# Four channel chunks in two visits: regrouping the half-height products of layer 0 inside the score loop of layer 1

## The chip, the cores and the metric

The kernel runs on one core of a Trainium2 chip, as one program that is launched once. The metric is the time of one execution on the device, in microseconds (us). The core has a matrix engine (TensorE, "PE" in the profile; its weight loads are listed apart as "PEld"), a vector engine (VectorE, "DVE"), a scalar engine (ScalarE, "ACT"), GpSimd ("POOL") and DMA queues. Each engine works through its own queue in order, and semaphores tie the queues together.

## The reference, cut to what matters

The input is x, 8 images of 512 channels and 1024 pixels. Four layers follow one another. The change touches the end of layer 0 and the start of layer 1:

```python
# layer 0, per image; f, g: 64 channels after batch norm and relu, h: 64 channels
z  = einsum('bcn,bcm->bnm', f, g)
z2 = einsum('bnm,bcm->bcn', z / largest_singular_value(z), h)
x  = conv1x1(z2, Wv, bv) + x
# layer 1: group norm over 32 groups of 16 channels, then attention over 1024 pixels
h  = group_norm(x)
q, k, v = conv1x1(h, wq), conv1x1(h, wk), conv1x1(h, wv)
x  = x + conv1x1(softmax(q^T k / sqrt(512)) v, wp)
```

Layer 2 is a second attention with 128 channels, and layer 3 is a 1x1 convolution with signs, a batch norm and a parametric relu. All sums must be those of the reference in float32.

## The kernel before

**Tiling.** Channels lie on 128 partitions in `CC` = 4 chunks, pixels in `NH` = 2 halves of 512. A product has 512 columns at most and goes to one of 8 PSUM banks (`bank()`). A float32 product shows in the trace as two passes, so two MATMUL records.

**An entry stage, then a steady part.** The entry stage (to about 192 us) reads all images for the batch norm of layer 0, prepares weights and brings the first image into layer 1. The steady part is `fast(env, n, hb, ua)`, called for n = 0 to 7, one image each in the order 6, 7, 0, 1, ... 5. In it an image runs through layers 1 to 3, and the end of layer 0 for the next image is woven in.

**The end of layer 0 for the next image is `enter` (line 399).** Layer 0 has been folded so that x becomes x + pv^T f + bias, with `pv` 64 x 512 (made by `weights0`, line 283, from the 64 x 64 matrix of the chain below) and `f` 64 x 1024. Only 64 of the 128 rows of the array are needed, so pixel half 0 uses rows 0 to 63 and pixel half 1 uses rows 64 to 127 (`side(h)`). For each of the 4 channel chunks, `enter` takes two banks and issues the two half-height products (line 408); VectorE adds them to x (line 417) and takes the statistics of the sum (line 420, gathered in line 421). Then it yields, so one chunk is one *visit*. After four visits there are two small steps with products by `gmat`, which average the statistics over the groups of 16 channels: the first is line 428 (VectorE prepares it in 427 and reads it in 429 to 432), the second is line 435, followed by the reciprocal root on GpSimd and VectorE. The results are the scale and shift of the group norm, which `normal` (line 447) applies at step 5 of `values1`, half-way through the image.

**The weights need two half-height products more, for every second image.** `entering` (line 855) loads f, makes sure that the chain of the image pair is finished, and for an even image calls `weights0` for both images of the pair (line 287, with copies to the tile `pv` by VectorE in line 290 and ScalarE in line 292). It then goes straight on to the first visit.

**The score loop is the clock.** `scores1` makes the 1024 x 1024 scores as 4 blocks of `seven` products (Strassen's scheme), so the loop in `fast` has 28 steps k = 0 to 27; at each one TensorE does 4 passes of 128 x 128 x 512 (line 385). Within a block of seven, two of the banks are accumulated over two steps with others between; at k = 6, 13, 20 and 27 a block ends. VectorE evicts four products of a block (lines 342 and 344), ScalarE the others and the exponentials, and the sums of the exponentials are two VectorE additions for each block (lines 529 to 532). `make_v` follows with 14 steps of the same length, then `values1` with 14 steps (line 552).

**Work is woven in by step.** At k = 8 `entering` starts; at k = 12, 15, 18, 21, 24 and 27 (`k >= 11 and k % 3 == 0`) one step of it is drawn: four visits, then the two group products. `chore(2)` draws, every second call, one step of the *chain*: 22 small steps for each image pair, which find the largest singular value of z by repeated squaring (two products of 128 x 128 in lines 1013 and 1014, evicted by VectorE or ScalarE, now and then a sum in line 1045). The three chains left for the steady part are used up in the first images.

**Queues.** The program order is a wish: the compiler's scheduler lays out the queue of each engine by its own estimates of when an operand is ready, and moves ready work ahead of what is not. Only the entry stage keeps TensorE in the order written (`tc.manual_schedule`).

Of the kernel before, what the change touches and what calls it, by code (L numbers as in the profile page):

```python
# [20 lines left out]
CC = C // P  # L21
NT = N // P
HF = 512
NH = N // HF
# [61 lines left out]
def kernel(  # L86
# [36 lines left out]
    def bank():  # L123
        return psum["bank"].tile([P, HF], F32, tag="bank", name="bank")
# [271 lines left out]

    weights = {}

    def enter(xt, f, pv):

        st = stat.tile([P, CC, NH, 6], F32, tag="st1", name="st1")
        mv = stat.tile([P, CC, 2], F32, tag="mv1", name="mv1")
        for oc in range(CC):
            banks = [bank() for h in range(NH)]
            for h, ps in enumerate(banks):
                mm(  # L408
                    out=ps,
                    lhsT=pv[side(h), bass.ts(oc, P)],  # L410
                    rhs=f[side(h), :],
                    start=True,
                    stop=True,
                )
            for h, ps in enumerate(banks):
                xs = xt[:, oc, half(h)]
                nc.vector.scalar_tensor_tensor(
                    xs, ps, bvo[:, oc : oc + 1], xs, ALU.add, ALU.add
                )
                nc.vector.bn_stats(st[:, oc, h, :], xs)  # L420
            nc.vector.bn_aggr(mv[:, oc, :], st[:, oc, :, :])
            yield

        ps = bank()
        mean = stat.tile([P, CC], F32, tag="mean1", name="mean1")
        dev = stat.tile([P, CC], F32, tag="dev1", name="dev1")
        nc.vector.tensor_tensor(mv[:, :, 0], mv[:, :, 0], bo, ALU.subtract)
        mm(out=ps[:, 0:CC], lhsT=gmat, rhs=mv[:, :, 0], start=True, stop=True)
        nc.vector.tensor_copy(mean, ps[:, 0:CC])
        nc.vector.tensor_tensor(dev, mv[:, :, 0], mean, ALU.subtract)  # L430
        nc.vector.tensor_tensor(dev, dev, dev, ALU.mult)
        nc.vector.tensor_tensor(dev, dev, mv[:, :, 1], ALU.add)
        yield
        ps = bank()
        mm(out=ps[:, 0:CC], lhsT=gmat, rhs=dev, start=True, stop=True)
        sc = rsqrt_eps(stat, ps[:, 0:CC], CC, "r1")
        bi = stat.tile([P, CC], F32, tag="bi1", name="bi1")
        nc.vector.tensor_tensor(sc, sc, vec("L1_conv_gamma"), ALU.mult)
        nc.vector.tensor_tensor(mean, mean, bo, ALU.add)
        nc.vector.tensor_tensor(bi, mean, sc, ALU.mult)  # L440
        nc.vector.tensor_tensor(bi, vec("L1_conv_beta"), bi, ALU.subtract)
        norm[:] = sc, bi
        yield
# [411 lines left out]
    def entering(n):  # L855

        b = order[n]
        f = load_f(b)

        def steps():  # L860
            while b // 2 not in ready:
                next(behind)
            if b % 2 == 0:
                for i in (b, b + 1):
                    pvs[i] = weights0(i)
            yield from enter(resident[b], f, pvs.pop(b))

        return steps()

# [3 lines left out]
    def fast(env, n, hb, ua):  # L873


        b = order[n]
        xt = resident.pop(b)
        more = n + 1 < B
        ahead = iter(())
        count = [0]  # L880

        def chore(every):
            count[0] += 1
            if count[0] % every == 0:
                next(behind, None)

        es = [None] * NT
        for k, _ in enumerate(scores1(env, hb, ua, es)):
            if rest3 and k % 2 == 0:
                if next(rest3[0], "end") == "end":  # L890
                    rest3.pop()
                    if more and order[n + 1] not in resident:
                        resident[order[n + 1]] = load_x(order[n + 1])
            if n == 0 and k == 2:
                weights["o"] = sums_of(quarters_of(wo, chunks, cols2), [so[:, i] for i in range(3)], True)
            if n == 0 and k == 6:
                tp = quarters_of(sbw["tpg"], chunks, [slice(0, P), slice(P, 2 * P)])
                weights["tp"] = sums_of(tp, [sp[:, i] for i in range(3)], True)
            if k == 8 and more:
                ahead = entering(n + 1)  # L900
            if k >= 11 and k % 3 == 0:
                next(ahead, None)
            if not rest3:
                chore(2)
        for _ in ahead:
            pass
        esum = es.pop()
        vt = env["big"].tile([P, NT, C], F32, tag="uv", name="vt")
        for k, _ in enumerate(make_v(hb, vt)):
            if k == 3:  # L910
                r = inverse_sums(env, esum, n)
            chore(2)
        scratch = env["big"].tile([P, 3, N], F32, tag="us", name="scratch")
        got = []
        steps = iter(())
        for k, _ in enumerate(values1(env, xt, vt, es, r, scratch)):
            chore(2)
            if k == 5 and more:
                nxt = resident[order[n + 1]]
                hb = split_h(env, normal(env, nxt))  # L920
        signs = None
        if more:
            steps = make_u(env, hb, got)
        else:
            signs = unpacked(env)

        def fill(k=1):
            for _ in range(k):
                next(steps, None)

        made = []
        for k, _ in enumerate(project2(env, xt, made)):
            fill(k > 5)
        tt, pt, gt = made
        es, esum = scores2(env, pt, tt, lambda t: fill(t % 2))
        banks, r = [None, None], None

        def values2(h, ts):
            if banks[h] is None:
                banks[h] = bank()  # L940
            for t in ts:
                mm(  # L942
                    out=banks[h],
                    lhsT=gt[:, t, :],
                    rhs=es[t][:, half(h)],
                    start=t == 0,
                    stop=t == NT - 1,
                )
            if t == NT - 1:
                att = env["small"].tile([P, HF], F32, tag="half_b", name="att")  # L950
                nc.vector.tensor_tensor(att, banks[h], r[:, h, :], ALU.mult)
                return att

        dst = channels(out[b])
        fill()
        values2(0, range(0, 2))
        if more:
            r = inverse_sums(env, esum, B + n)  # L960
            values2(0, range(2, NTH))
            att = values2(0, range(NTH, NT))
            values2(1, range(0, NTH))
            close2(xt, att, 0)
            att = values2(1, range(NTH, NT))
            fill()
            for _ in leave(env, xt, dst, [0]):
                fill()
            close2(xt, att, 1)
            rest3.append(leave(env, xt, dst, [1], stop=True))  # L970
            next(rest3[0])
            fill(2)
            for _ in steps:
                pass
        else:


            r = inverse_rows(env, esum, B + n)
            att = values2(0, range(2, NT))
            values2(1, range(0, 2))  # L980
            close2(xt, att, 0)
            values2(1, range(2, 6))
            before, after = leave(env, xt, dst, [0], signs), leave(env, xt, dst, [1], signs)
            count = count_bad(env)
            next(count)
            next(before)
            next(before)
            att = values2(1, range(6, NT))
            next(before)
            close2(xt, att, 1)  # L990
            for _ in before:
                pass
            next(after)
            next(count)
            for _ in after:
                pass

        return hb, got[0] if more else None
# [435 lines left out]
    with tc.manual_schedule(engines={mybir.EngineType.PE}):  # L1434
        steps = entering(0)
        for k, _ in enumerate(chain(jl, True)):

            for _ in range(4 if k == 3 * NSTEP + 3 else 2 if k != 1 and k % 3 < 2 else 1):
                next(todo, None)
            for args in (next(relus, None),):  # L1440
                if args:
                    relu(*args)
        for k in range(CC + 2):
            next(steps)
            for _ in range(3 if k < CC else 5):
                next(todo, None)
        for _ in todo:
            pass
# [193 lines left out]
```

## Time and profile before

| | before |
|---|---|
| time, median of three (range) | 1924.97 us (1924.53 to 1925.95) |
| span of the profiled execution | 1922.7 us |
| TensorE busy | 1897.7 us, 99% |
| VectorE busy | 1136.0 us, 59% |
| ScalarE, GpSimd busy | 509.5 us, 227.3 us |
| full-height products of 512 columns in the score loop (line 385) | 4 records of a step follow one another in 1.72 us |
| half-height products of `enter` (line 408) | 128 records in 32 visits of 4 records |
| addition of line 417, statistics of line 420 | 742 ns and 688 ns, 64 of each |

The page names the busy share of each engine over the span. A MATMUL record overlaps the next one (592 ns long, but the next starts 430 ns later), so the distance from one start to the next is what a product costs; the timeline by engine gives the starts. In the timeline, a row is a group of equal records in sequence: start, length, engine, line, tile and operands, number of records, and in brackets the idle time before it and who ended it. The list of waits gives, for each pair of waiting and releasing line, the sum, the number and the longest.

### The profile page before, as it was taken

To read this page: it belongs to the slowest core of one execution; us is meant where nothing else is said; L and a number is where in the kernel's file an instruction comes from. 1 tells how busy PE (TensorE), PEld (TensorE's weight loads), DVE (VectorE), ACT (ScalarE), POOL (GpSimd) and SP (SyncE) were. 2 spreads that over 40 slices of the span, in tenths; PEclk is the share of its full clock that TensorE was granted. 3 is DMA by queue.
4 is the path that set the end of the run, shared out by engine and by line. 5 is a ranking of instruction groups with operands and counts; after the bars stand their busy time and mean duration, and the time that the engine had idled before them with its cause. 6 is when DMAs were issued, how large, how long until landed. Compare 5 with 4: busy or idle time off the path is not lost.

```text
span 1922.7 us, 16428 instructions
## 1 busy us (share of the span) xinstructions
PE 1897.7 (99%) x6166; PEld 978.9 (51%) x6166; DVE 1136.0 (59%) x1761; ACT 509.5 (27%) x811; POOL 227.3 (12%) x175
## 2 busy tenths in 40 slices
PE   9999999999999999999999999999999999999997
PEld 3376456544655446444545446544645455544653
DVE  3246577448764677447754676447653775466547
ACT  2141222035212332024212431034202521143114
POOL 0000011200111001200121011201120011101121
PEclk9999999999999999999999999999999999999999
DMA  8420000002000120002000120002000200010001
GB/s 325 150 77 7 0 6 12 1 12 88 17 1 0 33 71 12 1 11 88 17 1 0 33 71 12 1 12 88 11 0 2 96 7 6 0 34 22 12 0 46
DMA packets 27783, 66.46 MB, mean 35 GB/s; under 512 B 4272, under 2 KB 5424, under 8 KB 27056
## 3 DMA queue, kind: packets, MB, share of 16 engines
q1 hardware_dynamic: 26768, 64.90, 10.0%
q8 instruction: 51, 0.84, 0.2%
q10 hardware_dynamic: 864, 0.43, 0.1%
q14 instruction: 36, 0.29, 0.1%
q0 software_dynamic: 64, 0.00, 0.0%
HBM read 38.51 MB, written 18.87 MB: 30 GB/s over the span
## 4 chain that ended last, share of the span: by engine, by line
PE 90%; DVE 8%; ACT 1%; issue 1%; DMA 0%; POOL 0%; DVEq 0%; ACTq 0%
PE bank L385 40%; PE bank L552 20%; PE bank L942 6%; PE bank L801 6%; PE bank L1234 4%; PE bank L653 3%; PE bank L408 2%; PE bank L670 2%; PE wide L1274 1%; DVE both L744 1%; DVE both L714 1%; PE wide L1321 1%; PE bank L1013 1%; PE bank L1014 1%; PE bank L693 1%
## 5 line engine op out<-in xcount | busy, mean ns | idle before, releaser
L552 PE MATMUL bank<-e,vt 128*128 128x512 f32 x768 | 333.8, 592 | 0.0
L552 PEld LDWEIGHTS bank<-e,vt 128*128 128x128 f32 x768 | 145.0, 190 | 175.4 <-issue 173.4
L385 PE MATMUL bank<-ut,h 128*128 128x512 f32 x384 | 181.5, 595 | 0.0
L385 PE MATMUL bank<-us,hs 128*128 128x512 f32 x256 | 121.9, 598 | 1.3 <-DVE us L314 0.5
L342 DVE TENSOR_TENSOR e<-bank,e 128x512 f32<-128x512 f32 x128 | 87.4, 683 | 57.1 <-PE bank L385 56.5
L942 PE MATMUL bank<-e,tpg 128*128 128x512 f32 x256 | 114.7, 595 | 0.0
L801 PE MATMUL bank<-tpg 128*128 128x512 f32 x256 | 114.6, 592 | 0.0
L385 PEld LDWEIGHTS bank<-ut,h 128*128 128x128 f32 x384 | 71.3, 190 | 84.8 <-issue 83.3
L808 ACT ACTIVATE e<-bank 128x512 f32<-128x512 f32 x128 | 76.4, 597 | 128.5 <-PE bank L801 128.5
L357 POOL TENSOR_TENSOR e<-e 128x512 f32<-128x512 f32 x32 | 44.1, 1379 | 413.1 <-ACT e L336 395.2
L385 PE MATMUL bank<-wo,h 128*128 128x256 f32 x384 | 91.9, 382 | 0.0
L813 DVE TENSOR_TENSOR esum<-esum,e 128x1024 f32<-128x1024 f32 x48 | 58.8, 1225 | 54.9 <-ACT e L808 54.9
L385 PE MATMUL bank<-h,wu 128*128 128x512 f32 x192 | 90.3, 593 | 0.7 <-ACT ut L347 0.7
L342 DVE TENSOR_TENSOR vt<-bank,vt 128x512 f32<-128x512 f32 x64 | 44.0, 688 | 65.8 <-PE bank L385 65.5
L942 PEld LDWEIGHTS bank<-e,tpg 128*128 128x128 f32 x256 | 48.1, 190 | 63.2 <-issue 63.1
L801 PEld LDWEIGHTS bank<-tpg 128*128 128x128 f32 x256 | 48.6, 190 | 60.8 <-issue 60.5
L385 PEld LDWEIGHTS bank<-wo,h 128*128 128x128 f32 x384 | 71.6, 190 | 14.3 <-ACT vt L336 4.9
L357 POOL TENSOR_TENSOR ut<-ut 128x512 f32<-128x512 f32 x16 | 21.8, 1360 | 479.0 <-ACT ut L338 479.0
L385 PEld LDWEIGHTS bank<-us,hs 128*128 128x128 f32 x256 | 46.7, 190 | 56.1 <-issue 46.4
L681 ACT ACTIVATE sg<-xt,rb 128x512 f16<-128x512 f32 x64 | 45.0, 718 | 103.7 <-DVE xt L672 100.2
L830 DVE RECIPROCAL rsum<-bank 128x512 f32<-128x512 f32 x15 | 50.4, 3357 | 30.1 <-PE bank L822 30.1
L653 PEld LDWEIGHTS bank<-tpg,xt 128*128 128x128 f32 x512 | 59.5, 192 | 7.2 <-issue 7.2
(328 smaller groups left out, 3037.2 us busy)
## 6 DMA issues: line engine op xcount, KB each, us to landing
xt<-in_x SPq DMA_DIRECT2D x55, 512.0 KB
out<-both SPq DMA_DIRECT2D x63, 256.0 KB
rfull<-rsum SPq DMA_DIRECT2D x60, 128.0 KB
f_dram<-f SPq DMA_DIRECT2D x8, 256.0 KB
fb<-f_dram SPq DMA_DIRECT2D x8, 256.0 KB
w<-in_w SPq DMA_DIRECT2D x1, 1024.0 KB
q<-in_w_q SPq DMA_DIRECT2D x1, 1024.0 KB
k<-in_w_k SPq DMA_DIRECT2D x1, 1024.0 KB
```

Source lines behind the costliest of these rows:

```text
L342: nc.vector.tensor_tensor(dst, ps, u, ALU.add)
L357: nc.gpsimd.tensor_tensor(c22, c22, c12, ALU.add)
L385: mm(out=ps[:, q * w : (q + 1) * w], lhsT=lt(ka, kb, q, k), rhs=rhs(ka, kb, q, k), start=first and q == 0 and k == 0, stop=last and k == 1 ...
L552: mm(out=ps, lhsT=a[:, t, bass.ts(r_, P)], rhs=e[t], start=first and t == 0, stop=last and t == NTH - 1, skip_group_check=True,)
L653: mm(out=ps[:, i, :], lhsT=xt[:, cc, bass.ts(4 * h + i, P)], rhs=sbw["tpg"][:, cc, 2 * P : 3 * P], start=cc == 0, stop=cc == CC - 1,)
L681: nc.scalar.activation(sg[:, cc, :], xt[:, cc, half(h)], AF.Sign, bias=rb3[:, cc : cc + 1])
L801: mm(out=ps, lhsT=pt[:, 0, bass.ts(t, P)], rhs=tt[:, 0, half(h)], start=True, stop=True,)
L808: nc.scalar.activation(e[:, half(h)], ps, AF.Exp, scale=float(P) ** -0.5)
L813: nc.vector.tensor_tensor(esum, esum, e, ALU.add)
L830: nc.vector.reciprocal(r, ps)
L942: mm(out=banks[h], lhsT=gt[:, t, :], rhs=es[t][:, half(h)], start=t == 0, stop=t == NT - 1,)
L1234: mm(out=banks[i][side(h), :], lhsT=w0[i][:, cc, :], rhs=xt[:, cc, half(h)], start=cc == 0, stop=cc == CC - 1,)
```

## The change

It has four parts. `enter` gets a parameter `visits`: with 2, a visit takes two channel chunks, so four banks and eight records of half-height products in sequence, and VectorE gets the four additions and statistics in one go. The steady part uses 2, the entry stage keeps 4. `entering` yields after `weights0`, so that these products are a step of their own. The steps of the score loop at which `entering` is drawn become k = 10 (weights), 13 and 20 (the visits, both at the end of a block of seven) and 27 (first group product); the second group product moves to step 5 of `make_v`. The chain is not drawn at k = 13, 14, 15, 20, 21 and 22. In the entry stage the filler steps are dealt out anew, because `entering` has a step more. The purpose is to have TensorE change between full-height and half-height products less often, and to leave time between the statistics and the products that need them.

```diff
-    def enter(xt, f, pv):
+    def enter(xt, f, pv, visits=CC):
...
-        for oc in range(CC):
-            banks = [bank() for h in range(NH)]
-            for h, ps in enumerate(banks):
+        n = CC // visits
+        for v in range(visits):
+            banks = [(oc, h, bank()) for oc in range(v * n, (v + 1) * n) for h in range(NH)]
+            for oc, h, ps in banks:
                 mm(
...
-            for h, ps in enumerate(banks):
+            for oc, h, ps in banks:
                 xs = xt[:, oc, half(h)]
...
-            nc.vector.bn_aggr(mv[:, oc, :], st[:, oc, :, :])
+                if h:
+                    nc.vector.bn_aggr(mv[:, oc, :], st[:, oc, :, :])
             yield
...
-            yield from enter(resident[b], f, pvs.pop(b))
+            yield
+            yield from enter(resident[b], f, pvs.pop(b), 2 if n else CC)
...
-            if k >= 11 and k % 3 == 0:
+            if k in (10, 13, 20, 27):
                 next(ahead, None)
-            if not rest3:
+            if not rest3 and k not in (13, 14, 15, 20, 21, 22):
                 chore(2)
-        for _ in ahead:
-            pass
...
             if k == 3:
                 r = inverse_sums(env, esum, n)
+            if k == 5:
+                next(ahead, None)
             chore(2)
+        for _ in ahead:
+            pass
...
-        for k in range(CC + 2):
+        for n in (2, 3, 3, 3, 3, 4, 6):
             next(steps)
-            for _ in range(3 if k < CC else 5):
+            for _ in range(n):
                 next(todo, None)
```

## The prediction

> **What bounds the kernel now.** I read the page first, busy shares and the chain that ended last, then the starts of TensorE's records around `enter`, then the waits.
>
> ```profile
> PE 1897.7 (99%) x6166; PEld 978.9 (51%) x6166; DVE 1136.0 (59%) x1761; ACT 509.5 (27%) x811; POOL 227.3 (12%) x175
> ...
> PE 90%; DVE 8%; ACT 1%; issue 1%; DMA 0%; POOL 0%; DVEq 0%; ACTq 0%
> ```
>
> TensorE is busy for 99% of the span and carries 90% of the chain. Only 1922.7 - 1897.7 = 25.0 us are idle. So a gain must come from the distance between products. The timeline of TensorE in the image n = 3 (no chain steps any more) shows it:
>
> ```profile
> 906.55 1.13 PE L287 MATMUL bank<-wv,gm 64*128 64x512 f32 x4
> 907.61 1.12 PE L385 MATMUL bank<-ut,hs 128*128 128x512 f32 x2
> 909.03 1.13 PE L408 MATMUL bank<-fb,pv 64*128 64x512 f32 x4 [0.30 <-ACT pv L292]
> ...
> 914.58 1.13 PE L408 MATMUL bank<-fb,pv 64*128 64x512 f32 x4
> 915.64 1.98 PE L385 MATMUL bank<-ut,h 128*128 128x512 f32 x4
> 917.46 1.88 PE L385 MATMUL bank<-us,hs 128*128 128x512 f32 x4
> 919.18 1.88 PE L385 MATMUL bank<-ut,h 128*128 128x512 f32 x4
> 920.99 1.13 PE L408 MATMUL bank<-fb,pv 64*128 64x512 f32 x4
> 922.05 1.99 PE L385 MATMUL bank<-us,h 128*128 128x512 f32 x4
> ...
> 931.99 1.88 PE L385 MATMUL bank<-us,hs 128*128 128x512 f32 x4
> 934.28 0.39 PE L428 MATMUL bank<-mv,gmat 128*128 128x4 f32 x2 [0.41 <-DVE mv L427]
> ```
>
> Read the first column as differences. An undisturbed step takes 919.18 - 917.46 = 1.72 us for 4 records, 0.43 us each. The step after a visit takes 917.46 - 915.64 = 1.82, so 0.10 too much; the step before the next one takes 920.99 - 919.18 = 1.81, so 0.09 too much. The visit itself takes 922.05 - 920.99 = 1.06 us. Its two halves run beside each other, so 4 records should cost what 2 full ones do, 0.86; 0.20 is too much. **A visit thus carries 0.10 + 0.09 + 0.20 = 0.39 us that are no arithmetic** (0.40 from the single records, which start 7 ns apart in each pair). All 28 visits of the steady part show this.
>
> Two waits belong to the same work:
>
> ```profile
> PE bank L428 <- DVE mv L427: 2.3, 5, 0.6
> PE bank L408 <- ACT pv L292: 1.6, 4, 0.7
> ```
>
> Five times the first group product waits for VectorE, and four times the first visit waits for the copy of `pv`.
>
> **What the Trainium skill says.** "TensorEngine Tiling (Array Packing)", section Key Properties: "Changing tiling mode (not just tile) drains the TensorE". The 0.09 before and 0.10 inside the end of each visit agree with a drain at either border. "TensorE: Matmul & The Clock Gate", section LDWEIGHTS: a load takes about 128 / 1.2 = 107 ns whatever the height. That is what lies open after each drain, since nothing was streaming to hide it: the rest of the 0.20 inside the visit and the 0.10 after it. The same page, Part 3 (The mechanism), has products of different row groups run concurrently, and weight loads hidden behind products of another row group; the 7 ns agree with the first, and no place in this trace has two pairs in sequence to show the second. "PSUM — Partial Sum Buffer" gives 8 banks; the code takes as many.
>
> **The change part by part.**
>
> 1. *Two chunks per visit.* Seven images (n + 1 = 1 to 7) have 4 visits each, later 2. Arithmetic stays. 14 visits go away, each with its two borders: 14 x 0.40 = **5.6 us**. Unknown is the border between the two chunks inside a visit: at best it costs nothing (0.86 us for the second chunk), at worst the weight load or the end drain shows again, up to 0.20 us, so 0 to 2.8 us over 14 visits. I take 0, because the height doesn't change there and the next weights can load while products stream, as they do between full products (0.43 us apart with 0.19 us weight loads).
>
> 2. *Weights three steps ahead of the first visit.* Before, 907.61 to 909.03 is 1.42 us for 2 records that should take 0.86 + 0.10 + 0.09 = 1.05: the wait costs 0.37. Afterwards 3 steps of 1.72 us = 5.2 us lie between; the two copies (0.69 and 0.57 us) need under 2. Saved in three images (n = 1, 3, 5): **1.1 us**. The borders of line 287 stay.
>
> 3. *Group products later.* VectorE in the same image, by its timeline:
>
> ```profile
> 933.40 0.20 DVE L421 BATCH_NORM_AGGREGATE mv<-st 128x2 f32<-128x12 f32 x1
> 933.52 0.64 DVE L572 TENSOR_TENSOR e<-e 128x512 f32<-128x512 f32 x1
> 934.07 0.15 DVE L427 TENSOR_TENSOR mv<-mv,bo 128x4 f32<-128x4 f32 x1
> ```
>
> The statistics are done 6 us after the fourth visit (927.40), but line 428 is due at 931.99 + 1.72 = 933.71 and starts at 934.28: 0.57 us late, plus 0.10 for its weights, which load in the open (its two records and what follows take 0.24 us in place of 0.14 where nothing waited). In n = 3 to 6 alike: 4 x 0.67 = **2.7 us**. Afterwards seven steps, 12.0 us, lie between the visit at k = 20 and line 428 at k = 27. In that time VectorE has 4 x (0.70 + 0.64) = 5.4 us for the visit (pairs take 1.40 and 1.28 us in the timeline), 0.4 for the aggregates, 2.4 for the exponential sums and 4 x 0.69 = 2.8 for evictions: 11.0 us, of which line 427 needs only the first 8 or so. The second group product has 6 further steps, and the scale is needed only after `make_v`; nothing waits for it.
>
> 4. *What is queued behind the bigger burst.* A visit puts 5.4 us on VectorE in one go, and behind it 2.4 us of exponential sums and the next block's first eviction, due 3.5 us after the visit but then reached after about 8 to 9. Who waits for that? Not the products of scores, whose operands are old. Only PSUM banks: at the end of a block one or two are unevicted, the visit takes four, the next block's four accumulators need one more at 0, 1.7, 3.4 and 5.2 us after the visit, while the burst frees one every 1.35 us. There are always one or two in hand. The burst is 11.0 us of work per 14 us from visit to visit, so VectorE catches up. Cost: 0. The next image has landed by then (its loads in n = 3 end near 905 us, the first visit comes at 911).
>
> 5. *Chain kept away.* Chain steps are deferred, not dropped. There are 3 x 22 = 66; n = 0 draws (56 - 6) / 2 = 25, enough for the 22 that n = 1 needs at k = 10, and n = 1 and 2 have room for the rest. A step costs TensorE 0.44 us wherever it stands. Cost: 0; the gain is only that no eviction of a chain step queues behind the burst.
>
> 6. *Entry stage.* Visits stay at four. At 161.68 the weights start and at 163.48 the first visit, 1.80 us against 0.86 to 1.06 for the pair, with TensorE waiting for `pv`; 0.8 us go. Two filler steps between cost a change of height out and in, 0.3 us by part 1 (the first weight load is open already). **0.5 us** saved; the wait at line 428 stays there.
>
> Sum: 5.6 + 1.1 + 2.7 + 0.5 = 9.9 us, so 1924.97 - 9.9 = **1915.1 us**.
>
> **The rivals.** *A: the visit doesn't stay whole or its inner border costs.* The scheduler put a product between lines 287 and 408 above, so it may part the eight records where its estimate has no bank free; or 0.20 us show per chunk. Part 1 falls to between 0 and 2.8: 1924.97 - 4.3 = 1920.7 to 1917.9. Against it: all present visits are whole. *B: the waits move.* VectorE's burst makes the first group product or a bank wait as now: parts 1 to 3 are given back by about 0.7 us at each of 14 visits, 9.8 us: 1924.9, no change. For it: 59% of VectorE's span is busy, but in this stretch 11 of 14 us. *C: slower.* If each burst keeps TensorE without a bank for one addition and statistics more, 1.35 us x 14 = 19 us against 9.9 won: 1934. Against it: the bank count in part 4, and no wait of TensorE for an eviction in this stretch today.
>
> **Chances.** Forecast 0.73, A 0.13, B 0.08, C 0.06. "Faster by over 0.2%" means below 1921.1: the forecast and A, 0.85 after a little of A is taken off; no change 0.08; slower 0.07. The range reaches from 1912, where the waits of chain steps at line 1013 (0.7 + 0.5 + 0.4 + 0.3 = 1.9 us in the list of waits) and the entry's 0.6 at line 428 go as well, to 1922, which takes in A.
>
> **What would show it.** In the timeline of TensorE: rows of line 408 with x8, about 1.92 us to the next start, two per image (right for part 1; 2.12 says that the inner border costs, two rows of x4 that the visit was parted). Line 287 and line 408 three steps apart with no wait for `pv` but none of 0.30 in brackets (part 2). Lines 428 and 435 with no idle time before them in n = 3 to 6 (part 3). No new row in the waits of lines 385 and 408 for VectorE's lines 417 or 420 (part 4). TensorE's sum of busy time should fall and its share stay at 99%. The prediction is wrong if such waits appear, or if the distance at each border was not due to the change of height.

## The result and the profile after

| | before | after |
|---|---|---|
| time, median (range) | 1924.93 us (1924.53 to 1925.95) | 1914.91 us (1914.62 to 1916.04) |
| ratio, 95% interval | | 0.9948 (0.9931 to 0.9965) |
| span of the profiled execution | 1922.7 us | 1912.8 us |
| first records: start of the 12th MATMUL | 8.5 us | 9.2 us |
| entry, from line 287 to the first product of `make_u` | 30.67 us | 31.34 us |
| steady part, from there to the end | 1730.36 us | 1719.06 us |

The forecast of 1915.1 us holds. The last three rows split the 9.9 us of the spans: the steady part gained 11.3, the entry lost 0.67, and 0.7 went in the first ten microseconds, where both kernels have the same instructions (in the runs below the 12th record starts anywhere between 8.5 and 9.5 us). **So the total hides two misses of opposite sign**: the steady part gained 1.9 us more than forecast, the entry 1.2 less. That these and the 0.7 of the start cancel is luck. I use the length of the steady part below to compare kernels: where the queue is the same it repeats to 0.1 to 0.2 us, which the whole time doesn't. From the first product of `values1` in one image to that in the next, two kernels with the same queue agree to 0.01 us; differences "per image" are taken there.

The page of the kernel after, busy shares and the chain that ended last:

```profile
PE 1891.3 (99%) x6166; PEld 980.3 (51%) x6166; DVE 1126.5 (59%) x1761; ACT 510.4 (27%) x811; POOL 224.5 (12%) x175
...
PE 92%; DVE 6%; issue 1%; ACT 1%; DMA 0%; POOL 0%; DVEq 0%; ACTq 0%
```

TensorE has as many instructions as before and is busy 6.4 us less; idle time went from 25.0 to 21.5 us. The distance between records counts as busy where records overlap, so most of the gain shows as busy time, not as idle time.

The timeline of TensorE in the image n = 3 of the kernel after (line 408 is now 409, line 428 is 430, line 435 is 437):

```profile
899.73 1.13 PE L287 MATMUL bank<-wv,gm 64*128 64x512 f32 x4
900.79 1.98 PE L385 MATMUL bank<-ut,h 128*128 128x512 f32 x4
...
904.32 1.88 PE L385 MATMUL bank<-ut,hs 128*128 128x512 f32 x4
906.13 1.99 PE L409 MATMUL bank<-fb,pv 64*128 64x512 f32 x8
908.05 1.98 PE L385 MATMUL bank<-ut,h 128*128 128x512 f32 x4
909.87 1.88 PE L385 MATMUL bank<-us,hs 128*128 128x512 f32 x4
...
918.46 1.88 PE L385 MATMUL bank<-ut,hs 128*128 128x512 f32 x4
920.27 1.99 PE L409 MATMUL bank<-fb,pv 64*128 64x512 f32 x8
...
932.59 1.88 PE L385 MATMUL bank<-ut,hs 128*128 128x512 f32 x4
934.30 0.28 PE L430 MATMUL bank<-mv,gmat 128*128 128x4 f32 x2
934.44 1.97 PE L385 MATMUL bank<-wo,h 128*128 128x256 f32 x8
```

Line 409 stands whole, x8, twice per image. A visit takes 908.05 - 906.13 = 1.92 us, where one chunk took 1.06: the second chunk costs 0.86, the price of its arithmetic. The borders are as before: 906.13 - 904.32 = 1.81 ahead and 909.87 - 908.05 = 1.82 behind. The weights and the first visit are three steps apart with no idle time in brackets. The group product follows its predecessor after 934.30 - 932.59 = 1.71 us, and what comes next starts 0.14 us after it, in place of 0.24: no wait.

VectorE in the same stretch of the kernel after (line 420 is now 421, line 427 is 429):

```profile
914.65 0.68 DVE L342 TENSOR_TENSOR e<-bank,e 128x512 f32<-128x512 f32 x1
...
915.91 0.69 DVE L342 TENSOR_TENSOR e<-bank,e 128x512 f32<-128x512 f32 x1
...
929.37 0.20 DVE L423 BATCH_NORM_AGGREGATE mv<-st 128x2 f32<-128x12 f32 x1
...
930.65 0.16 DVE L429 TENSOR_TENSOR mv<-mv,bo 128x4 f32<-128x4 f32 x1
```

Line 429 is through 3.5 us before line 430 is due. The two rows of line 342 are VectorE's evictions of the second and third product of the block that begins at 908.05; they come late, behind the burst, and nobody waits for them. That of the third product will matter in the experiments.

In the list of TensorE's waits of the kernel after, the entry has one new row and keeps one:

```profile
PE quad L1133 <- DVE xt L418: 0.7, 1, 0.7
...
PE bank L430 <- DVE mv L429: 0.6, 1, 0.6
```

### The profile page after: what moved, and what is told of

It reads as the page before. It is cut to its first block, busy times and chain, and to the rows that moved or that the text cites. A ratio compares the mean times of both kernels' runs of the same rounds, so it can differ in the third digit from the quotient of the medians.

```text
span 1912.8 us, 16430 instructions
## 1 busy us (share of the span) xinstructions
PE 1891.3 (99%) x6166; PEld 980.3 (51%) x6166; DVE 1126.5 (59%) x1761; ACT 510.4 (27%) x811; POOL 224.5 (12%) x175
## 4 chain that ended last, share of the span: by engine, by line
PE 92%; DVE 6%; issue 1%; ACT 1%; DMA 0%; POOL 0%; DVEq 0%; ACTq 0%
PE bank L385 42%; PE bank L554 20%; PE bank L949 6%; PE bank L803 6%; PE bank L1241 5%; PE bank L655 3%; PE bank L409 2%; PE bank L672 2%; PE wide L1281 1%; DVE both L746 1%; PE wide L1328 1%; DVE both L716 1%; PE bank L1020 1%; PE bank L1021 1%; PE bank L695 1%; PE bank L824 1%
## 5 line engine op out<-in xcount | busy, mean ns | idle before, releaser
L1241 PE MATMUL bank<-xt,fg 128*64 128x512 f32 x256 | 59.4, 611 | 4.3 <-DMA fg<-in_w_fg 4.3
```

Source lines behind the costliest of these rows:

```text
L1241: mm(out=banks[i][side(h), :], lhsT=w0[i][:, cc, :], rhs=xt[:, cc, half(h)], start=cc == 0, stop=cc == CC - 1,)
```

## The experiments

All times are medians; the kernel before had 1925.1 to 1925.5 us in the same series. "Steady" is the length of the steady part from the trace.

### One chunk per visit again

```diff
-            yield from enter(resident[b], f, pvs.pop(b), 2 if n else CC)
+            yield from enter(resident[b], f, pvs.pop(b), CC)
...
-            if k in (10, 13, 20, 27):
+            if k in (10, 13, 16, 20, 23, 27):
```

> The changed kernel, but each visit takes one channel chunk again (k = 13, 16, 20, 23); weights at 10, group products and chain as in the change. If the gain is the number of changes of height: 14 more visits x 0.40 us, 1914.9 + 5.6 = 1920.5 us, and in the trace 28 visits of 1.06 us, each with 0.09 before and 0.10 after. If the gain came from the other parts (waits, chain): about 1914.9. Line 430 is due 4 steps, 7 us, after the last visit and should not wait.

Measured: 1919.84 us, ratio to before 0.9973 (0.9963 to 0.9984); steady 1724.72 us, so 5.66 us more than the kernel after. Of these, 0.13 lie behind the last visit, where the queues are the same; in each of the seven images the run takes 0.78 to 0.80 us more, so 0.39 to 0.40 for each visit that came back. Part 1 of the forecast is shown.

### Full-height products in the visits

```diff
-                    lhsT=pv[side(h), bass.ts(oc, P)],
-                    rhs=f[side(h), :],
+                    lhsT=pv[:, bass.ts(oc, P)] if visits == 2 else pv[side(h), bass.ts(oc, P)],
+                    rhs=f if visits == 2 else f[side(h), :],
```

> The changed kernel, but in the steady part the products of line 408 use all 128 rows of pv and f (so both pixel halves get the sum of the two halves' products, which is not the reference). No change of height is left at the visits, but halves no longer run beside each other: 8 products of 0.86 us = 6.87 us in each image in place of two visits of 1.92 + 0.19 = 4.22. If the borders are due to the change of height: + 2.65 x 7 = 18.5 us, 1933.4 us, with 1.72 us for the steps before and after a visit. If any visit has such borders, whatever its height: another 2 x 0.40 x 7 = 5.6 us, 1939.

Measured: 1932.75 us, 1.0040 (1.0027 to 1.0054); steady 1737.29 us, 18.2 more than after, against 18.5 expected; per image it is 2.63 to 2.64 us, against 2.65. The timeline of TensorE in this run:

```profile
911.66 1.88 PE L385 MATMUL bank<-ut,hs 128*128 128x512 f32 x4
913.38 3.60 PE L409 MATMUL bank<-fb,pv 128*128 128x512 f32 x8
916.82 1.88 PE L385 MATMUL bank<-ut,h 128*128 128x512 f32 x4
918.53 1.88 PE L385 MATMUL bank<-us,hs 128*128 128x512 f32 x4
```

1.72, 3.44, 1.71: the same visit at full height has no border at all. The 0.40 us belong to the change of height, not to a change of line, operands or banks. (Half-height products come in side-by-side pairs throughout this kernel, and the run takes away both at once; whether a half-height product alone has the same border isn't shown.)

### The chain beside the visits again

```diff
-            if not rest3 and k not in (13, 14, 15, 20, 21, 22):
+            if not rest3:
```

> The changed kernel, but the chain is drawn at every step k, also beside the visits. By my forecast (part 5 costs and brings nothing): 1914.9 us. By the trace after, where the idle time ahead of lines 1013 and 1045 of before (1.4 and 0.3 us in the first three images) is gone: 1.7 us come back, 1916.6 us. If the bigger burst on VectorE holds up every chain step behind it (two visits in each of three images, some 3 us each): 1914.9 + 18 = 1933 us at most.

Measured: 1921.96 us, 0.9983 (0.9977 to 0.9990); steady 1725.55, 6.5 more than after. Rows of its list of TensorE's waits that the kernel after lacks:

```profile
PE bank L1020 <- DVE cur L1042: 2.7, 2, 1.9
PE bank L1052 <- DVE tj L1048: 1.2, 2, 0.6
...
PE bank L1020 <- DVE half__2945 L1067: 1.0, 1, 1.0
```

The first two rows, 3.9 us in four waits, are chain products that wait for a small VectorE instruction, which stands in the queue behind the burst. The third stands at 533 us in `make_v`, far behind the visits, where VectorE itself waits for ScalarE and GpSimd. The value lies between the two that were expected: more than what the kernel before lost to its single visits, less than a burst at every visit.

### The chain kept away in the kernel before

```diff
-            if not rest3:
+            if not rest3 and not 12 <= k < 24:
                 chore(2)
```

> The kernel before, with one edit: the chain is not drawn at k = 12 to 23, where its single visits stand. By my forecast (part 5 brings nothing): no change, 1925.2 us. By the trace, where 1.4 us of distance ahead of line 1013 and 0.3 ahead of line 1045 vanished with the change: 1.7 us less, 1923.5 us.

Measured: 1934.36 us, 1.0045 (1.0031 to 1.0059); steady 1738.92, 8.6 *more* than before. Both expectations miss. The chain is deferred further than in the change (12 steps of 28, not 6) and ends only in the image n = 3, right ahead of the weights. TensorE, and below it ScalarE, in that run:

```profile
912.10 1.13 PE L287 MATMUL bank<-wv,gm 64*128 64x512 f32 x4
913.16 1.13 PE L385 MATMUL bank<-ut,hs 128*128 128x512 f32 x2
917.04 1.13 PE L408 MATMUL bank<-fb,pv 64*128 64x512 f32 x4 [2.76 <-ACT pv L292]
```

```profile
910.27 0.60 ACT L363 ACTIVATE e<-bank 128x512 f32<-128x512 f32 x1 [1.13 <-PE bank L385]
910.88 1.28 ACT L1089 ACT_TABLE_LOAD   x1
912.18 0.21 ACT L1089 ACTIVATE ln<-tr 128x8 f32<-128x8 f32 x1
912.40 1.28 ACT L1092 ACT_TABLE_LOAD   x1
...
915.46 1.06 ACT L527 ACTIVATE e<-e 128x1024 f32<-128x1024 f32 x1 [1.56 <-DVE e L342]
916.42 0.57 ACT L292 COPY pv<-bank 128x512 f32<-128x512 f32 x1
```

The end of a chain needs a logarithm and an exponential, each with a table load of 1.28 us on ScalarE. VectorE waits for their results, its eviction of line 342 comes late, ScalarE's line 527 waits 1.56 us for that, and the copy of `pv` stands behind all of it. That wait and one of 1.3 us ahead of line 1013 explain about half of the 8.6 us; the rest is spread and wasn't taken apart. What follows: keeping the chain away has no fixed price. It pays or costs by where the deferred steps land.

### The first group product three steps after the last visit

```diff
-            if k in (10, 13, 20, 27):
+            if k in (10, 13, 20, 23, 27):
...
-            if k == 5:
-                next(ahead, None)
```

> The changed kernel, but the group products are drawn at k = 23 and 27, three steps after the last visit, as before the change. The statistics of the second visit are done 9.3 us after its start in the trace after, the product would be due 7.1 us after it: a wait of about 2.2 to 3.5 us in each of 7 images, 1914.9 + 15 to 25 = 1930 to 1940 us, so that two chunks at a time alone would lose. Rival: the wait is that of before, 0.67 us in four images: 1917.6. If the group product can wait without TensorE: 1914.9.

Measured: 1927.85 us, 1.0015 (1.0008 to 1.0021); steady 1732.44, 13.4 more than after and slower than before. Timeline of TensorE, then of VectorE, in n = 3:

```profile
932.15 3.60 PE L385 MATMUL bank<-ut,h 128*128 128x512 f32 x8
937.22 1.13 PE L385 MATMUL bank<-ut,hs 128*128 128x512 f32 x2 [1.47 <-DVE e L342]
938.18 0.28 PE L430 MATMUL bank<-mv,gmat 128*128 128x4 f32 x2
```

```profile
936.48 0.68 DVE L342 TENSOR_TENSOR e<-bank,e 128x512 f32<-128x512 f32 x1
937.09 0.15 DVE L429 TENSOR_TENSOR mv<-mv,bo 128x4 f32<-128x4 f32 x1
```

The size is somewhat below what was expected, 1.9 us per image; the place is not where it was expected. The scheduler moved other products ahead of line 430, among them the first half of the seventh product of the block (`ut,hs`), and that one waits, 1.47 us in each of 7 images, for the eviction at 936.48. Why it must is settled below. Line 429 ends only at 937.09 + 0.15 = 937.24, so the group product could not have started before that either. With a burst of this size, the merge without the later group product is no gain.

### The weights drawn with the first visit

```diff
-            if k in (10, 13, 20, 27):
+            if k == 13:
+                next(ahead, None)
+            if k in (13, 20, 27):
                 next(ahead, None)
```

> The changed kernel, but the weights (line 287) are drawn at k = 13 together with the first visit, as they were before. By part 2 of the forecast the wait for the copies comes back in three images: + 3 x 0.37 = 1.1 us, 1916.0 us. Rival: with eight records in the visit, the scheduler puts more full-height products between, a border more or less: between 1914.9 and 1916.5.

Measured: 1916.58 us, 0.9955 (0.9941 to 0.9968); steady 1721.19, 2.1 more than after. TensorE's wait at line 409 for the copy by line 292 is back, now 2.6 us in three times where the steady part of the kernel before had 0.3 each. Moving the weights ahead is worth at least the 1.1 us of part 2, and twice that once the visit stands at the end of a block.

### The entry stage dealt as before

```diff
-            yield
+            if n:
+                yield
             yield from enter(resident[b], f, pvs.pop(b), 2 if n else CC)
...
-        for n in (2, 3, 3, 3, 3, 4, 6):
+        for k in range(CC + 2):
             next(steps)
-            for _ in range(n):
+            for _ in range(3 if k < CC else 5):
```

> The changed kernel, but the entry stage is dealt as before (no step between the weights and the first visit there). By my forecast (part 6 saves 0.5 us): 1915.4 us. By the trace after, where the stage from the weights product to the first product of layer 1 takes 0.67 us longer than before: 1914.2 us, with the wait of 0.7 us for line 418 at line 1133 gone and that for the copy of pv back.

Measured: 1913.67 us, 0.9942 (0.9929 to 0.9956), with the entry at 30.67 us and the steady part as in the kernel after. So the new entry costs 0.67 us. The timelines of TensorE show the exchange, the kernel before first:

```profile
161.68 1.13 PE L287 MATMUL bank<-wv,gm 64*128 64x512 f32 x4
163.48 1.13 PE L408 MATMUL bank<-fb,pv 64*128 64x512 f32 x4 [0.67 <-ACT pv L292]
```

and the kernel after:

```profile
162.37 1.13 PE L287 MATMUL bank<-wv,gm 64*128 64x512 f32 x4
163.43 2.05 PE L1328 MATMUL wide<-gt,ht 128*128 128x128 f32 x16
165.41 1.13 PE L409 MATMUL bank<-fb,pv 64*128 64x512 f32 x4
...
168.76 0.66 PE L1133 MATMUL quad<-ident,g 128*128 128x128 f32 x4 [0.72 <-DVE xt L418]
```

The wait for `pv` is filled, but a filler further on (line 1133, transposes) now waits as long for a PSUM bank that line 418 has not read yet (the entry has only four such banks), and a change of height was added.

### Four chunks in one visit

```diff
-            yield from enter(resident[b], f, pvs.pop(b), 2 if n else CC)
+            yield from enter(resident[b], f, pvs.pop(b), 1 if n else CC)
...
-            if k in (10, 13, 20, 27):
+            if k in (10, 13, 27):
```

> The changed kernel, but one visit takes all four chunks (eight banks, 16 records at k = 13; nothing at 20; group products at 27 and in make_v as in the change). Border theory with enough banks: one visit less in each of 7 images, 7 x 0.40 = 2.8 us, 1914.9 - 2.8 = 1912.1. Bank theory: the visit wants all eight banks while one or two are unevicted, and VectorE then has 10.8 us of additions and statistics in one go; the next block's accumulators come 3.6, 5.4, 7.1 and 8.8 us after its start. One addition with its statistics (1.35 us) lost per image is 9.5 us: 1921.6. Chain steps drawn at k = 16 and 18 may queue behind the burst in the first three images: up to 3 us each.

Measured: 1926.60 us, 1.0007 (0.9999 to 1.0015), no gain left. In its trace two chain products wait 2.1 and 2.3 us behind the burst, in the first two images, as was feared. The same with the old entry and the chain away from k = 13 to 18:

> A candidate: four chunks in one visit at k = 13 as in the run before, chain kept away at k = 13 to 18, and the entry stage dealt as before the change, which by itself gave 1913.7. If the border theory holds and the banks suffice: 1913.7 - 2.8 = 1910.9 us. If the banks don't suffice: 1913.7 - 2.8 + 9.5 = 1920.4 us.

Measured: 1921.23 us, 0.9979 (0.9971 to 0.9987); 1.33 us more per image than after from n = 3 on. By the numbers this is what "the banks don't suffice" asks for. The timelines of this run, TensorE and VectorE, say otherwise:

```profile
907.28 3.70 PE L409 MATMUL bank<-fb,pv 64*128 64x512 f32 x16
910.92 1.98 PE L385 MATMUL bank<-ut,h 128*128 128x512 f32 x4
...
919.61 1.88 PE L385 MATMUL bank<-us,h 128*128 128x512 f32 x4
922.95 1.98 PE L385 MATMUL bank<-ut,hs 128*128 128x512 f32 x4 [1.47 <-DVE e L342]
```

```profile
920.95 0.68 DVE L342 TENSOR_TENSOR e<-bank,e 128x512 f32<-128x512 f32 x1
...
922.21 0.69 DVE L342 TENSOR_TENSOR e<-bank,e 128x512 f32<-128x512 f32 x1
```

The visit runs whole, 16 records in 910.92 - 907.28 = 3.64 us, and so do the next six products. Only the seventh stops, for 1.6 us, until the second row of line 342 ends at 922.90. In `seven` the third product opens the bank `pd`, VectorE reads it half-way (`plus(vd, None, c21, c22)`), and the seventh product adds to the same bank. It may not start before that read: in each of the seven images it starts 0.05 us after the read ends. (Three banks of a block are read half-way and added to later, not two, as the part on the kernel before has it; ScalarE reads the other two.) The wait of 1.62 us and 0.10 for a weight load in the open, less one border of 0.40, make 1.32 of the 1.33 us per image. By this reading the wait is for an accumulator, not for a free bank; the next run tests it.

### ScalarE reads the accumulator half-way

```diff
-        plus(vd, None, c21, c22)
+        if exp is None:
+            plus(vd, None, c21, c22)
+        else:
+            nc.scalar.copy(c22, vd)
+            nc.vector.tensor_tensor(c22, c22, c21, ALU.add)
```

On the run with four chunks and the old entry:

> The run with four chunks in one visit and the old entry (1921.2), with one edit: in the blocks of seven of the score loop, the half-way read of the accumulator pd (third product) is a copy by ScalarE, and VectorE adds from SBUF. If TensorE waited there because the seventh product may not add to pd before VectorE has read it: the wait of 1.47 us per image goes and the borders' gain shows, 1913.7 - 2.8 = 1910.9 us. If it waited for a free bank (eight taken by the visit, as my rival C had it): the wait stays, about 1921.

Measured: 1913.11 us, 0.9936 (0.9922 to 0.9949). Its timeline of TensorE:

```profile
906.78 3.70 PE L413 MATMUL bank<-fb,pv 64*128 64x512 f32 x16
...
919.11 1.88 PE L389 MATMUL bank<-us,h 128*128 128x512 f32 x4
920.82 1.88 PE L389 MATMUL bank<-ut,hs 128*128 128x512 f32 x4
```

The visit takes the same eight banks, VectorE has the same burst, and the seventh product follows after 1.71 us. From n = 3 on an image now takes 0.40 us less than after, one border. The accumulator theory is shown, the bank theory is out. On two chunks, where nobody waited for that read, the same edit should do nothing:

> The same edit on the run with two chunks per visit and the old entry (1913.7), where no product waited for that read. Both theories: 1913.7 us, since ScalarE (27% busy) has room for 32 copies of 0.6 us more and TensorE waits for nothing here. If ScalarE's exponentials fall behind: some us more.

Measured: 1913.60 us, 0.9941 (0.9927 to 0.9954), as without it (1913.67). ScalarE has room for the copies.

### Four chunks, ScalarE's read, and the chain kept away longer

The four-chunk run still had chain steps behind the burst in the first images. With `not 13 <= k <= 21` as the rule for the chain:

> A candidate: four chunks in one visit, ScalarE reading pd half-way, old entry (1913.1), with the chain kept away until VectorE is through the burst, at k = 13 to 21. If what is left between that run and the border theory's 1910.9 is chain steps queued behind the burst (in its trace 1.3 us of waits at line 1025 and 0.9 us in the first image): 1913.1 - 1.5 = 1911.6 us. If the chain now ends later, beside the weights of image n = 3, as in the run on the kernel before: some us more, up to 1918.

Measured: 1911.65 us, 0.9931 (0.9917 to 0.9944); steady 1717.08, 2.0 less than after. The chain now ends in the image n = 3, but 10 us ahead of the weights, and nothing waits for it there. The three edits together (one visit, ScalarE's read, chain away until the burst is through) give these 2.0 us, the old entry 0.67; the medians, from different series, are 3.3 us apart.

## Why the prediction was right, and where not

| part | forecast | measured | by |
|---|---|---|---|
| 1 two chunks per visit | -5.6 us | -5.5 to -5.7 | one chunk per visit again |
| 2 weights earlier | -1.1 | -1.1 | wait of 0.37 gone three times in the trace |
| 3 group products later | -2.7 | -2.7 | lateness gone in n = 3 to 6 in the trace |
| 4 bigger burst | 0 | 0 | no new wait for it in the steady part |
| 5 chain kept away | 0 | -1.8 to -2.0 | no run of its own: what is left of 11.3 in the steady part |
| 6 entry | -0.5 | +0.67 | entry dealt as before |

**Right:** the steps that were read from distances between starts. The images without chain steps show them nearly alone: n = 4 and 6 gained 1.47 us each, 0.79 for two visits fewer and 0.68 for the group product, and n = 5 gained 1.84, with 0.37 for the weights. The border of 0.40 us came out of three subtractions in one timeline; that it is due to the change of height was taken from the Trainium skill ("TensorEngine Tiling (Array Packing)", Key Properties) and is now shown by the full-height run. The unknown inner border, bounded at 0 to 0.20 us per chunk, is 0: the second chunk takes 0.86 us. The weight loads are thus hidden between pairs of the same height, which no trace of before could show. Rival A did not occur: all 14 visits are whole.

**Wrong, part 5.** "Cost: 0; the gain is only that no eviction of a chain step queues behind the burst" counted the chain's own instructions and overlooked that VectorE already delayed them in the kernel before. There, line 1013 comes late twice, both times in the first image:

```profile
254.25 1.88 PE L385 MATMUL bank<-us,hs 128*128 128x512 f32 x4
256.79 0.49 PE L1013 MATMUL bank<-cur 128*128 128x128 f32 x2 [0.66 <-DVE cur L1035]
...
281.87 1.89 PE L385 MATMUL bank<-so,hs 128*128 128x256 f32 x8
284.23 0.46 PE L1013 MATMUL bank<-cur 128*128 128x128 f32 x2 [0.47 <-DVE r_e L235]
```

The distances, 2.54 and 2.36 us in place of 1.72 and 1.73, are 1.4 us too long together; in the kernel after none is. In the first case the eviction of line 1035 stands behind the additions and statistics of a visit, in the second behind the root of the second group product, which waits for GpSimd. With 0.3 us at line 1045, behind a visit of the third image, that is 1.7 us, near the 1.8 to 2.0 that the sum leaves. The part can't be tied to the rule for the chain alone: the change moved visits and group products as well, the same kind of rule made the kernel before slower, and drawing the chain beside the bursts cost 6.5 us.

**Wrong, part 6.** The sum took the idle time of 0.8 us as won and 0.3 us as the border. The missing term is the filler's need of a bank, 0.7 us at line 1133: filling one wait moved the same VectorE delay to another instruction.

**Right in the result, wrong in the reason: part 4 and rival C.** I wrote that the products of the score loop wait for no eviction, "Only PSUM banks". They can: in each block the seventh product needs the half-way read of `pd`. In the kernel after that read ends at 915.91 + 0.69 = 916.60 and the seventh product starts at 918.46, so there were 1.9 us to spare, the least in any image; in the kernel before it was 4 us or more. Two chunks fit, four did not. The forecast had this margin by luck.

Part 3 was understated in its role: without it the change would have lost (1927.85 us), since the burst outlasts three steps. The two edits are one.

## What to carry to other kernels

Read the price of a change of tile height off the distances between starts, just ahead of and behind the odd instruction, and group the odd ones until the next resource stops you. When grouping makes a burst for another engine, list every instruction that needs something from that engine *later in its queue*: small consumers (group products, chain steps) and accumulators that are read half-way and added to again; free banks are only one of these. Then move the consumers away from the burst or the read to another engine, and look where the moved work lands.

## What the runs showed of the hardware

A change between full-height and half-height float32 products costs about 0.20 us in each direction: some 0.09 ahead of the first record of the new height and 0.10 behind it (14 visits more cost 0.39 to 0.40 us each). The drain and the open weight load of the prediction fit the two pieces; no run here tells them apart. Within one height, pairs of half-height products follow one another without extra, 0.86 us for four further records (16 in sequence take 3.64 us), and the two halves of a pair start 7 ns apart. A product that adds to a bank which VectorE has still to read started 0.05 to 0.06 us after the end of that read (seven waits in the run with four chunks and the old entry, seven in the one with the early group product). A table load on ScalarE took 1.28 us, twice at the end of each chain, and it started when the instruction ahead of it ended (910.27 + 0.60 = 910.87), as did the ACTIVATE after it (910.88 + 1.28 = 912.16, next start 912.18); the Trainium skill ("ScalarE: Activation LUTs", What ACT_TABLE_LOAD costs) has the same 1283 ns but a drain of 1380 ns on top, which doesn't show here. Identical first instructions reached the 12th MATMUL between 8.5 and 9.5 us from run to run, more than several of the effects studied here.
